# Starting the head inside layer 3 and feeding it chunk by chunk, in a Fourier-layer image kernel

## The chip, the cores and the metric

The kernel runs on one core of one Trainium2 chip. The metric is the device time of one execution in microseconds; the time given for the kernel before is the median of three executions.

## What is computed

The input is eight images of eight channels, 256 x 256 pixels, float32. Two residual layers follow each other; each normalises its input per group of channels first. The first is a Fourier neural operator in four groups (two input channels and ten hidden channels each), the second a 3 x 3 dilation. Cut to what matters:

```python
h = _gconv1x1(concat(x, grid), fc0_w, fc0_b)            # 4 groups: 2+2 -> 10 channels
for i in range(4):
    h1 = _spectral_conv(h, sp_w1[i], sp_w2[i])          # 24 x 12 low modes of a 2-d FFT
    h2 = _gconv1x1(h, w_w[i], w_b[i])                   # 10 -> 10 per pixel
    h = h1 + h2
    if i < 3: h = _gswish(h, betas[i])
h = _gswish(_gconv1x1(h, fc1_w, fc1_b), betas[3])       # "head": 10 -> 128 per pixel and group
y = _gconv1x1(h, fc2_w, fc2_b)                          # "head": 128 -> 2

x = x + L0(_gn(x))                                      # layer 0, above
x = x + L1(_gn(x))                                      # layer 1: max over 3 x 3 windows
```

## The kernel before

**Rows and chunks.** The 256 rows of an image are dealt as 128 pairs of rows, n = 0 to 127. A pair of 512 pixels sits in one of NBLK = 3 blocks of 10 channels on the partitions of a group, in one of NQ = 4 columns, of one of NCH = 11 chunks of the tile `h`. A *state* is one column of one chunk, 128 partitions x 512 numbers, and holds up to three pairs. There are 44 states for the 128 pairs. Before the change, `_row_of` deals pair n to column n // 32, chunk (n % 32) // 3 and block n % 3 within the 32; a state order that follows n therefore walks all 11 chunks of column 0 first, then all of column 1, and so on.

**Layers.** `layers` runs, for each image, four layers. A layer takes the spectrum (`spectrum_h`), multiplies the modes (`mix`, DVE), turns them into rows (`rows_of`, PE `p_g` at L465/L471), and then `layer` runs 11 bursts, one for each chunk: 48 matmuls into `p_z` (L550/L553 and L556) and two ACT evictions into `h` (L561, in layer 3 L563). Layers 0 to 2 also transform each chunk back (`turn` L504, `transform` L521 to L525, `gather` L535). Layer 3 instead stores each chunk to DRAM as soon as it is made (`stored[c]`, 1,024 KB, L565), and beside it the next image's first spectrum is worked out (the generator `side`, which is `start(b + 1)`: `spectrum_x`, then `mix` of layer 0).

**The head.** For each image, `head` returns `first` and `second`. A `first` step, written *f* here, takes one pair n: it loads the state three further on (`load_state`, L752, 256 KB, SP queue, four buffers), does four matmuls from `hs` into PSUM (L776, 32 rows deep) and two ACT evictions with Silu into `act` (L777 and L778). A `second` step, *c*, takes two pairs: eight matmuls from `act` (L793) into one PSUM bank; `sum_up` later adds that bank to the rows of the image `y` on DVE (L800 for the first of eight, L802 for the others). After every eighth *c* there are statistics (L805 or L808) and a store of the finished rows. An image has 128 *f* and 64 *c*. In this text f1.0 is the first step *f* of image 1.

**The tail.** After the 64th *c* of an image, its `dilate` generator is put into `tails`. Each call makes one small piece of DVE work. For each of eight bands of rows the pieces are: fetch of the band (`yin`, POOL queue, 512 KB, L829), nothing, first maximum `m` (L840, waits for the fetch), second maximum (L842), vertical maximum (L845, L846), and then the subtraction, residual sum and store (L849 to L857) together with the next band's fetch. `yin` has one buffer.

**The order is written out by hand.** Nothing is scheduled: every generator yields strings, and the main loop plays them. "f" and "c" are steps of the oldest head that has one left, "C" is a *c* whose sum is put off, "t" is one call of the tail. The engines run their instructions in exactly that order. In layer 3 each chunk yields "fct" (up to chunk 7, then "fc") and "f"; `REST` holds the five strings that are played between layer 3 of one image and layer 0 of the next, another set for image 0 than for the rest. When no head is left in the layers, a last loop plays "ffc" and one tail call until the last image's head is through:

```python
        while heads:
            for kind in "ffc":
                if heads:
                    step(kind)
            tail()
```

`ready` (L579, L580) marks three chunks of layer 3 after which the first three states are asked for, and the first rows of `y` with the second of them. `stored`, yielded after layer 3, puts the new head into `heads`; until then, in image 0, no head exists, and `alone[0]` is true. For the last image `y` and the dilation live in `h` itself (`ya`, in chunks 0 to 2, `ma` and `oa` behind it), since `h` is free by then; `head` clears the border of `ya` on POOL.

Of the kernel before, what the change touches and what calls it, by code (L numbers as in the profile page):

```python
# [33 lines left out]
NBLK = 3  # L34
NCH = 11
NQ = 4
# [3 lines left out]
DR = 2  # L40
STEPS = 128
BEHIND = mybir.DependencyInfo(mybir.DependencyClass.Sync, mybir.DependencyReason.DATA)
REST = ("ff", "f", "f", "fC", "fc"), ("f", "fc", "ffC", "ff", "fc")


@with_exitstack
def fno_dilate_kernel(ctx: ExitStack, tc: tile.TileContext, a: dict, out: bass.AP):
# [11 lines left out]
    def ps_a(name):  # L59
        return ps.tile([128, 512], F32, tag="one", bufs=2, name=name)  # L60
# [4 lines left out]
    def ps_four(name):  # L65
        one, tri = ps_a(f"{name}_0"), ps_tri(f"{name}_1")
        return one, tri, [one] + [tri[:, i, :] for i in range(3)]

    def part(i):
        return slice(32 * i, 32 * i + 32)  # L70
# [132 lines left out]
    alone = [True]  # L203
# [182 lines left out]
    def load_sw(l, k):  # L386
        t = sb.tile([128, G, 2 * WID, WID], F32, tag="sw", bufs=3)
        nc.sync.dma_start(t.rearrange("p g m i -> p (g m i)"), a["spw"][l, k])
        return t
# [102 lines left out]
    def read_x(b, c):  # L492
        if b < n_img:
            for g in range(G):
                nc.sync.dma_start(h[32 * g : 32 * g + 6, c].rearrange("p f w -> p (f w)"), a["xp"][b, c, g])

    def layer(b, l, out_, stored, side, ahead):
# [73 lines left out]
        if l == 3:  # L571
            for c in range(NCH):
                burst(c)
                yield "fct" if c < 8 else "fc"
                next(side, None)
                if c + 1 < NCH:
                    yield "f"
                next(side, None)
                if c in ((3, 4, 5) if alone[0] else (6, 8, 9)):  # L579
                    yield "ready"  # L580
                if 0 < c < 4 and b + 1 < n_img:
                    ahead.setdefault("sw", []).append(load_sw(0, c - 1))
                if c > 3 and not alone[0]:
                    read_x(b + 1, c - 4)
            return
        for k in range((NCH + 1) // 2):
            c = 2 * k
# [48 lines left out]
    def start(b, out_):  # L636
        if b < n_img:
            if b == 0:
                out_["sw"] = [load_sw(0, k) for k in range(3)]
            yield from spectrum_x(b, out_)  # L640
            yield from mix(b, 0, out_)

    def rest(b, then):
        c = 0 if b == 0 else NCH - 4
        for n, _ in enumerate(then):
            yield REST[b > 0][n]
            for _ in range(2 if b == 0 else 1):
                if c < NCH:
                    read_x(b + 1, c)
                    c += 1  # L650
        for i in range(c, NCH):
            read_x(b + 1, i)
# [67 lines left out]
    def now_or_later(f):  # L720

        if held[0] is None:
            f()
        else:
            held[0].append(f)
# [14 lines left out]
    def head(b, stored, stats):  # L740
        hs, acts, box, done = {}, {}, {}, [0, 0]
        last = b + 1 == n_img
        if last:
            for t in (ya[:, :, 0:1], ya[:, :, HW + 1 :], ya[:, 0, :], ya[:, 17, :]):
                nc.gpsimd.memset(t, -BIG)

        def load_state(k):

            if k < NQ * NCH:
                j, c = k // NCH, k % NCH  # L750
                hs[k] = sb.tile([128, PIX], F32, tag="hs", bufs=4, name=f"hs_{b}_{k}")
                now_or_later(lambda: nc.sync.dma_start(hs[k], stored[c][:, PIX * j : PIX * (j + 1)]))  # L752

        def load_y(t):

            if t < 8:
                if last:
                    y = ya[:, 1 + 2 * t : 3 + 2 * t, 1 : HW + 1]
                else:
                    y = sb.tile([128, 512], F32, tag="yp", name=f"y_{b}_{t}")  # L760
                    y = y.rearrange("p (s w) -> p s w", s=2)
                box[t] = y
                now_or_later(lambda: nc.sync.dma_start(
                    y, a["x"][b].rearrange("c (p t s w) -> (c p) t s w", p=16, t=8, s=2)[:, t]))

        def first():

            n = done[0]
            done[0] += 1
            if n % 32 % NBLK == 0:  # L770
                load_state(n // 32 * NCH + n % 32 // NBLK + 3)
            k, blk = n // 32 * NCH + n % 32 // NBLK, n % 32 % NBLK
            act = sb.tile([128, G, 512], F32, tag="act", bufs=4, name=f"act_{b}_{n}")
            one, tri, banks = ps_four(f"p_fc1_{b}_{n}")
            for g in range(G):
                mm(banks[g], w1[part(g), blk, :], hs[k][part(g), :], start=True, stop=True)  # L776
            nc.scalar.activation(act[:, 0, :], one, AF.Silu)  # L777
            nc.scalar.activation(act[:, 1:4, :], tri, AF.Silu)  # L778
            acts[n] = act

        def second():

            n = 2 * done[1]
            done[1] += 1
            t, rb = n // 16, n % 16
            if rb == 8:
                load_y(t + 1)
            y, acc = box[t], ps_a(f"p_fc2_{b}_{n}")
            sums = acc.rearrange("p (s w) -> p s w", s=2)
            for i in range(2):  # L790
                act = acts.pop(n + i)
                for g in range(G):
                    mm(acc[part(g), :], w2[:, g, 15 - rb - i : 47 - rb - i], act[:, g, :],  # L793
                       start=i == 0, stop=i == 1)
            sums_due.append(lambda: add(t, rb, y, sums))

        def add(t, rb, y, sums):

            if rb == 0:
                nc.vector.scalar_tensor_tensor(y, sums, b2, y, ALU.add, ALU.add)  # L800
            else:
                nc.vector.tensor_tensor(y, sums, y, ALU.add)  # L802
            if rb == 14 and last:
                for i in range(2):
                    nc.vector.bn_stats(stats[:, 2 * t + i, :], y[:, i])  # L805
                dilate_early(t)
            elif rb == 14:
                nc.vector.bn_stats(stats[:, t, :], y.rearrange("p s w -> p (s w)"))  # L808
                whole = y_rows[b % 2][:]
                nc.gpsimd.dma_start(  # L810
                    bass.AP(whole.tensor, whole.offset + (1 + 2 * t) * HW, [[16 * HW, 128], [HW, 2], [1, HW]]), y)

        def ahead(n):

            load_state(n)
            if n == 1:
                load_y(0)

        return done, first, second, ahead


# [38 lines left out]
    heads, tails = [], []  # L860
# [16 lines left out]
    def tail():  # L877
        if tails and next(tails[0], tails) is tails:
            tails.pop(0)

    stats_of = {}
    with tc.manual_schedule(engines={PE, DVE, ACT, SP}):
        d = {}
        for _ in start(0, d):
            pass
        for b in range(n_img):
            stored = [dram.tile([128, NQ * PIX], F32, tag=f"hs{c}", name=f"stored_{b}_{c}") for c in range(NCH)]
            nxt, new, n_ready = {}, None, 0
            for n in layers(b, stored, d, start(b + 1, nxt), nxt):
                if n == "ready":  # L890
                    if new is None:
                        if b + 1 < n_img:
                            stats_of[b] = sb.tile([128, 8, 6], F32, tag="bn_y", name=f"bn_y{b}")
                        else:
                            stats_of[b] = spare[:, 16384:16480].rearrange("p (n s) -> p n s", s=6)
                        new = head(b, stored, stats_of[b])
                    new[3](n_ready)
                    n_ready += 1
                elif n == "stored":
                    heads.append((b, new))  # L900
                    alone[0] = False
                else:
                    for kind in n or "":
                        if kind == "t":
                            tail()
                        elif heads:
                            step(kind)
            d = nxt
# [5 lines that stand above are left out]
        for t in tails:  # L914
            for _ in t:
                pass
# [7 lines left out]
def _row_of():  # L924

    rows = np.full((NBLK, NQ, NCH, 2), -1)
    for n in range(HW // 2):
        j, c, blk = n // 32, n % 32 // 3, n % 32 % 3
        rows[blk, j, c] = 16 * (n % 16) + 2 * (n // 16) + np.arange(2)
    return rows  # L930


# [147 lines left out]
```

## Time and profile before

| | us |
|---|---|
| median of three executions (lowest, highest) | 3749.41 (3743.65, 3750.35) |
| the profiled execution, device time | 3748.67 |
| its span, first to last instruction | 3746.9 |
| mean granted TensorE clock | 0.978 |
| layer 3 of image 0, first burst to last (PE) | 305.6 to 341.2 |
| head of image 0: first step f | 341.07 |
| last burst of image 7 ends, last loop begins | about 3441.6 |
| last step f starts | 3716.38 |

A table of groups gives the instructions by line; its first rows are the head: L778 ACT 1493.3 us, L776 PE 1133.8 us, L793 PE 1008.7 us, L777 ACT 616.5 us. Engines are PE (matmul), PEld (weight load), DVE, ACT and POOL; SP only issues DMAs. In a timeline, a line has the start, the duration, the engine, the source line, the operation, output and input tiles, and in brackets the idle time before it and who ended it. In a table of waits, a line has the waiting instruction, the one it waited for, the total, the number of waits and the longest.

### The profile page before, as it was taken

What the parts mean: (1) busy time and instruction counts of PE and PEld (TensorE: products, weight loads), DVE (VectorE), ACT (ScalarE), POOL (GpSimd) and SP (SyncE); (2) the same over time, 40 slices, a digit from 0 to 9 for tenths busy, and PEclk for the clock granted to TensorE, in tenths of its full rate; (3) what the DMA queues carried; (4) which work ended last, traced back from release to release, by engine and by line L of the source; (5) the groups of instructions that cost most, each with busy time, mean ns of one, the idle gap of its engine ahead of it and who ended that gap; (6) DMA issues with size and microseconds to landing.
All of it is one profiled execution on the core that took longest, in us unless ns stands there. A gap on an engine that the chain in (4) does not pass through costs nothing.

```text
span 3746.9 us, 117677 instructions
## 1 busy us (share of the span) xinstructions
PE 3526.2 (94%) x53432; PEld 1287.2 (34%) x53432; DVE 2412.8 (64%) x3753; ACT 2836.0 (76%) x2947; POOL 117.0 (3%) x202
## 2 busy tenths in 40 slices
PE   5768999999999999999999999999999999999997
PEld 2323333333333333333333333333333333333222
DVE  6776656557775667756776577765777566772543
ACT  2435878777778777887787877878787877788886
POOL 1000000000000000000000000000000000000000
PEclk7878999999999999999999999999999999999998
DMA  3005211442225222262123612244222522225221
GB/s 89 16 15 198 60 46 44 149 123 63 74 81 180 82 61 71 85 211 64 50 68 112 192 55 71 58 155 131 63 74 79 180 85 60 71 63 188 81 85 48
DMA packets 114067, 344.91 MB, mean 92 GB/s; under 512 B 15984, under 2 KB 18480, under 8 KB 98144
## 3 DMA queue, kind: packets, MB, share of 16 engines
q1 hardware_dynamic: 95392, 276.32, 24.3%
q0 software_dynamic: 18176, 61.07, 4.9%
q8 instruction: 420, 6.88, 0.8%
q14 instruction: 79, 0.65, 0.1%
HBM read 213.33 MB, written 123.74 MB: 90 GB/s over the span
## 4 chain that ended last, share of the span: by engine, by line
PE 72%; DVE 16%; issue 5%; ACT 5%; DMA 2%; POOL 0%; ACTq 0%; DVEq 0%; POOLq 0%
PE p_fc L793 19%; PE p_fc L776 18%; PE p_z L556 9%; PE p_z L553 7%; PE p_d L521 7%; PE p_z L550 3%; DVE y L802 3%; DVE turned L504 3%; PE p_u L535 3%; DVE S L402 3%; DVE turned L399 2%; PE p_g L471 2%; DMA yin<-y_rows 2%; DVE turned L360 1%; ACT act L778 1%
## 5 line engine op out<-in xcount | busy, mean ns | idle before, releaser
L778 ACT ACTIVATE act<-p_fc 128x1536 f32<-128x1536 f32 x1024 | 1493.3, 1458 | 0.0
L776 PE MATMUL p_fc<-hs,c_w 32*128 32x512 f32 x8192 | 1133.8, 625 | 41.8 <-DVE y L802 20.8
L793 PE MATMUL p_fc<-act,c_w 128*32 128x512 f32 x8192 | 1008.7, 600 | 0.2 <-ACT act L778 0.2
L777 ACT ACTIVATE act<-p_fc 128x512 f32<-128x512 f32 x1024 | 616.5, 602 | 323.0 <-PE p_fc L776 311.5
L504 DVE STREAM_TRANSPOSE turned<-h 128x1024 f32<-128x1024 f32 x528 | 632.5, 1225 | 182.9 <-ACT h L561 182.3
L561 ACT ACTIVATE h<-p_z 128x512 f32<-128x512 f32 (+1 forms) x528 | 511.9, 1022 | 223.9 <-PE p_z L556 223.9
L802 DVE TENSOR_TENSOR y<-p_fc,y 128x512 f32<-128x512 f32 x392 | 267.9, 683 | 530.7 <-PE p_fc L793 530.7
L776 PEld LDWEIGHTS p_fc<-hs,c_w 32*128 32x128 f32 x8192 | 356.5, 183 | 614.1 <-ACT act L777 253.3
L793 PEld LDWEIGHTS p_fc<-act,c_w 128*32 128x32 f32 x8192 | 222.0, 109 | 694.5 <-issue 317.2
L556 PE MATMUL p_z<-c_binv,zt 32*128 32x256 f32 x5632 | 409.6, 404 | 0.0
L553 PE MATMUL p_z<-h,c_wt 32*32 32x512 f32 x8448 | 373.5, 604 | 8.4 <-ACT act L777 4.2
L556 PEld LDWEIGHTS p_z<-c_binv,zt 32*128 32x128 f32 x5632 | 258.7, 186 | 309.2 <-issue 296.2
L521 PE MATMUL p_d<-turned,c_fw 32*32 32x480 f32 (+1 forms) x9216 | 308.7, 541 | 0.7 <-DVE turned L504 0.4
L525 ACT ACTIVATE turned<-p_d 128x1440 f32<-128x1440 f32 x144 | 182.9, 1270 | 90.7 <-PE p_d L521 87.5
L563 ACT ACTIVATE h<-p_z,c_bias 128x512 f32<-128x512 f32 (+1 forms) x176 | 186.5, 1110 | 76.1 <-PE p_z L556 75.9
L402 DVE TENSOR_REDUCE S<-turned 128x80 f32<-128x800 f32 x192 | 188.9, 984 | 5.9
L399 DVE TENSOR_TENSOR turned<-t,B 128x800 f32<-128x800 f32 x192 | 188.7, 983 | 0.9
L209 DVE COPY zt<-p_g 128x264 f32<-128x264 f32 x276 | 145.1, 614 | 63.8 <-PE p_g L471 36.5
L521 PEld LDWEIGHTS p_d<-turned,c_fw 32*32 32x32 f32 x9216 | 127.4, 103 | 166.0 <-issue 65.0
L360 DVE STREAM_TRANSPOSE turned<-zt 128x960 f32<-128x960 f32 x96 | 176.9, 1870 | 2.5
L553 PEld LDWEIGHTS p_z<-h,c_wt 32*32 32x32 f32 x8448 | 94.5, 103 | 187.8 <-DVE y L802 54.1
L535 PE MATMUL p_u<-turned,c_stack 128*32 128x480 f32 (+1 forms) x1152 | 136.7, 543 | 11.9 <-DVE turned L524 6.2
(186 smaller groups left out, 1715.5 us busy)
## 6 DMA issues: line engine op xcount, KB each, us to landing
stored<-h SPq DMA_DIRECT2D x88, 1024.0 KB
hs<-stored SPq DMA_DIRECT2D x352, 256.0 KB
t<-in_spw SPq DMA_DIRECT2D x96, 400.0 KB
yin<-y_rows POOLq DMA_DIRECT2D x56, 512.0 KB, 5.1
h<-in_xp SPq DMA_DIRECT2D x352, 48.0 KB
turned<-in_xw SPq DMA_DIRECT2D x16, 1024.0 KB
y<-in_x SPq DMA_DIRECT2D x56, 256.0 KB
y_rows<-y POOLq DMA_DIRECT2D x56, 256.0 KB, 3.9
```

Source lines behind the costliest of these rows:

```text
L399: nc.vector.tensor_tensor(pr, sw[k], bt[:, k2, k].unsqueeze(2).to_broadcast([128, G, 2 * WID, WID]), ALU.mult)
L402: nc.vector.tensor_reduce(s[k2][:, k].rearrange("p s o g -> p (s o) g"), pr.rearrange("p g m i -> p m g i"), AX.X, ALU.add,)
L504: nc.vector.transpose(dst[:, 2 * i : 2 * i + 2], h[:, c, 2 * i : 2 * i + 2].rearrange("p f (s x) -> p f s x", s=2))
L521: mm(banks[q][part(v % 4), : 240 * n], fw8[part(q), v, :], t[part(q), :, :, v, : NBLK * WID], start=v < 4, stop=v >= 4)
L553: mm(o, wt[part(q), l, g, :], h[part(q), c, f, :], start=True, stop=False)
L556: mm(banks[q][:, HW * s : HW * (s + 1)], zt[part(q), 2 * c + s].rearrange("p f o -> p (f o)"), binv[part(q), :], start=False, stop=s == 1)
L561: nc.scalar.activation(dst, src, AF.Silu)
L776: mm(banks[g], w1[part(g), blk, :], hs[k][part(g), :], start=True, stop=True)
L777: nc.scalar.activation(act[:, 0, :], one, AF.Silu)
L778: nc.scalar.activation(act[:, 1:4, :], tri, AF.Silu)
L793: mm(acc[part(g), :], w2[:, g, 15 - rb - i : 47 - rb - i], act[:, g, :], start=i == 0, stop=i == 1)
L802: nc.vector.tensor_tensor(y, sums, y, ALU.add)
```

## The change

`place(n)` deals the pairs: three to a state, twelve to a chunk for chunks 0 to 9, and the last eight, two to a state, to chunk 10. `_row_of`, `load_state` and `first` use it, so the head walks all four columns of chunk 0, then of chunk 1, and so on; it needs chunk c only from pair 12c on. The host's tables follow `_row_of`. `ready` comes after chunks 2, 3 and 4 in every image (before: 3, 4, 5 in image 0 and 6, 8, 9 in the others). The head is put into `heads` at the first `ready` (after chunk 2), in image 0 at the third (after chunk 4) with two steps *f* at once, no longer at `stored`. `REST` is one set for all images.

```diff
-REST = ("ff", "f", "f", "fC", "fc"), ("f", "fc", "ffC", "ff", "fc")
+REST = "f", "fc", "ffC", "ff", "fc"
+def place(n):
+    full = NBLK * NQ * (NCH - 1)
+    if n < full:
+        return divmod(n, NBLK)
+    k, blk = divmod(n - full, 2)
+    return NQ * (NCH - 1) + k, blk
...
-                if c in ((3, 4, 5) if alone[0] else (6, 8, 9)):
+                if c in (2, 3, 4):
                     yield "ready"
...
-            yield REST[b > 0][n]
+            yield REST[n]
...
-                j, c = k // NCH, k % NCH
+                c, j = k // NQ, k % NQ
...
-            if n % 32 % NBLK == 0:
-                load_state(n // 32 * NCH + n % 32 // NBLK + 3)
-            k, blk = n // 32 * NCH + n % 32 // NBLK, n % 32 % NBLK
+            k, blk = place(n)
+            if blk == 0:
+                load_state(k + 3)
...
                     new[3](n_ready)
                     n_ready += 1
+                    if n_ready == (1 if b else 3):
+                        heads.append((b, new))
+                        if b == 0:
+                            step("f")
+                            step("f")
                 elif n == "stored":
-                    heads.append((b, new))
                     alone[0] = False
...
-        j, c, blk = n // 32, n % 32 // 3, n % 32 % 3
-        rows[blk, j, c] = 16 * (n % 16) + 2 * (n // 16) + np.arange(2)
+        k, blk = place(n)
+        rows[blk, k % NQ, k // NQ] = 16 * (n % 16) + 2 * (n // 16) + np.arange(2)
```

## The prediction

> **What bounds the kernel now.** I read the page first: busy times, the slices, the chain. Then PE's waits from 372 to 3440 us, then three stretches one by one.
>
> ```profile
> PE 3526.2 (94%) x53432; PEld 1287.2 (34%) x53432; DVE 2412.8 (64%) x3753; ACT 2836.0 (76%) x2947; POOL 117.0 (3%) x202
> ...
> PE   5768999999999999999999999999999999999997
> ...
> PE 72%; DVE 16%; issue 5%; ACT 5%; DMA 2%; POOL 0%; ACTq 0%; DVEq 0%; POOLq 0%
> ```
>
> PE is the bound. Its free time lies in the first three slices (image 0, layers 0 to 2, where no head can exist) and hardly anywhere else. The change does not reach those slices: before chunk 4 of layer 3 of image 0 its order is the old one. So it moves work from the last loop into a place that already has a 9 or 8.
>
> ```profile
> PE p_fc L776 <- DVE y L802: 20.6, 40, 1.8
> PE p_fc L776 <- DVE turned L524: 5.7, 6, 1.4
> PE p_u L535 <- DVE y L800: 4.8, 6, 1.2
> PE p_z L553 <- DVE y L802: 1.6, 6, 0.3
> ```
>
> These are the main waits of the seven later images that DVE causes. The last three come six times, once for each image whose layers carry a dilation; they will matter below. No wait of PE names a state load (`hs`) or a store.
>
> **What the change moves.** I compared the order in which both built programs issue on PE. The multiset of matmuls is the same. From the first spectrum matmul of image 1 on, the head is 14 *f* and 7 *c* ahead of its old place: 20 *f* and 9 *c* between chunk 4 of image 0 and `p_f` of image 1, where 6 and 2 stood. One image's cycle holds 128 *f* before and after, so the lead is carried unchanged through all images, and the last loop has 57 full rounds of f, f, c in place of 64. The sum is therefore: seven rounds at the end, against 14 *f* and 7 *c* in image 0, and what the shift does to DVE between.
>
> **Gain at the end.** The last loop's rounds:
>
> ```profile
> 3499.30 2.02 PE L776 MATMUL p_fc<-hs,c_w 32*128 32x512 f32 x16
> 3501.25 2.26 PE L793 MATMUL p_fc<-act,c_w 128*32 128x512 f32 x16
> 3503.44 2.02 PE L776 MATMUL p_fc<-hs,c_w 32*128 32x512 f32 x16
> ```
>
> Start to start 4.14 us; seven rounds are 29.0 us. Three rounds of the loop are late because eighth *c*, statistics and a piece of the dilation meet on DVE (they start 5.2, 7.9 and 5.3 us apart, 6.0 us lost). The tail now has four calls done when the loop begins, and by counting rounds I get four such meetings, one a shorter piece: +1 us (0 left: -6; one more at the mean of 2: +3). Gain at the end: 28.
>
> **Cost in image 0.** This is the step that decides. Two stretches, both from the end of chunk 4's burst in layer 3 to `p_f` of the next image: image 0 before, and image 1 before, which holds 20 *f* and 10 *c* among the same bursts and spectrum steps.
>
> ```profile
> core 0: us, PE busy (x) PEld busy (x) DVE busy (x) ACT busy (x) POOL busy (x), PEclk, DMA share, GB/s
> 321.76:354.83 33.07, 31.60 (x433) 12.67 (x429) 20.13 (x37) 25.82 (x27) 0.00 (x0) 1.00 0.91 360
> 736.36:796.15 59.79, 57.36 (x672) 19.88 (x664) 25.09 (x45) 51.02 (x54) 1.31 (x2) 1.00 0.68 210
> ```
>
> Image 0 after is image 1 before less one *c*. A *c* is 1.87 us here (eight matmul pairs, start to next start), so 57.9 us; less 33.07 is 24.8 us of cost. The free PE time in 33.07 us is only 1.47 us; the rest of what is regained comes from ACT pace, seen next: four *f* in a row went at 1.83 us each, where *f* with *c* between goes at 1.07.
>
> ```profile
> 343.50 1.61 PE L776 MATMUL p_fc<-hs,c_w 32*128 32x512 f32 x8 [0.31 <-ACT h L563]
> 345.33 1.61 PE L776 MATMUL p_fc<-hs,c_w 32*128 32x512 f32 x8 [0.22 <-ACT act L778]
> ```
>
> The two steps put in by hand are again *f* after *f*: +0.8.
>
> [...]
>
> **The first state.** The wait that the change adds: f0.0 needs state 0, which is loaded on SP's queue behind three stores of 1,024 KB and a 400 KB load; the trace has no load this close behind its store. The stores begin at 313.6 us and the DMA moves some 400 GB/s there (360 in the row, share 0.91), so 3.6 MB end at about 323, and the 256 KB state at 323.5 plus its completion; f0.0 is due at 325.0. Estimate +1 us, from 0 to 2.6 (one store at that rate). Queued behind f0.0 on PE is the burst of chunk 5, whose eviction releases the next store; nothing else waits for it.
>
> **Edits costed at nothing.** The order of states: the 352 loads keep size and number and are asked for three states (nine *f*) ahead; if that cover went, each would cost part of a store's 2.6 us. The earlier loads pass in front of some stores and `in_xp` loads on SP; the buffers they need were last read by PE a chunk earlier, so SP is not held up. In later images states 2 and 3 change places on SP; both are asked for at chunk 4, over a chunk before they are due. The last image's four border clears go to POOL (3% busy) four chunks earlier and wait there for the stores of chunks 0 to 2; `y` is loaded behind them. `REST` for image 0 is what the other images play already and is in the second row.
>
> **What the shift does to DVE.** This is the unknown part. The 45 calls of a dilation now start in layer 3 and stand four calls further on at each place. Where fetch and first maximum fall on the first and third call of one group of chunks, DVE stands in its queue:
>
> ```profile
> 1083.99 0.69 DVE L856 TENSOR_TENSOR o<-o,yin 128x512 f32<-128x512 f32 x1
> ...
> 1090.47 1.22 DVE L840 TENSOR_TENSOR m<-yin 128x1024 f32<-128x1024 f32 x1 [2.97 <-DMA yin<-y_rows]
> ...
> 1093.54 1.01 PE L535 MATMUL p_u<-turned,c_stack 128*32 128x480 f32 x8 [0.74 <-DVE y L800]
> ```
>
> Queued behind L840 are two transposes and the sum that frees a PSUM bank; PE waits 0.74 us for that, so some 2.2 of the 2.97 us are covered. Before, an image has one such place (layer 2) and a looser one (layer 1: DVE 1.97, PE 1.38 us). Counting calls through DVE's order, after it has two of the tight kind, in layers 0 and 1, and no looser one. The three rows of waits above sum to 12.1 us; in their place I put 6 x 2 x 0.8 = 9.6 (4.8 us over six): -2.5 us. Bounds: nothing left, -12.1; each at the longest of such waits, 1.4, is 16.8: +4.7. I take the tight row, since the order is the same instruction by instruction.
>
> [...]
>
> **Sum.** -29.0 + 1 + 24.8 + 0.8 + 1 - 2.5 = -3.9. On the profiled execution, 3748.67, that is 3744.8; its time stands 0.7 below the median. I say 3745. Bounds: -29.0 - 6 + 24.8 - 12.1 = -22 and -29.0 + 3 + 24.8 + 0.8 + 2.6 + 4.7 = +7, hardly ever reached together.
>
> **Rivals.**
> 1. *DVE's stalls go away* (the fetch lands in time at its new places): -3.9 - 9.6 = -13.5, 3735. For it: L840 waited for its fetch only 13 times out of 56. Against: the new places are as tight as the one that waits 2.97. Chance 0.17.
> 2. *The head falls into idle PE time*: 28 us, 3721. For it: weight loads are busy 12.67 and ACT 25.82 of 33.07 us. Against: the second stretch. Chance 0.06.
> 3. *The tight stalls pass to PE* (slower): the twelve new ones meet a fetch that lands 7.5 us after the end of L856, as the looser one in layer 1 did (964.2 to 971.76 us), in place of 5.8 (1084.7 to 1090.47); DVE then stands 4.6 us, 2.4 beyond the cover. 12 x 2.4 = 28.8 for 9.6: +15, 3764. It is slower beyond doubt once each costs PE over 1.75 us. For it: fetches of both lengths are in the trace. Against: 2.97 cost only 0.74. Chance 0.13.
> 4. *Head and stores collide in every image*: state 0 late by one store in eight images, 8 x 2.6 - 4 = +17, 3766; in images 1 to 7 two chunk periods of 6.7 us lie between the load and its use. Chance 0.03.
> That the head does not start earlier at all is excluded by the order on PE.
>
> **Chances.** The forecast has 0.61. About 0.2% (7.5 us) is what a measurement of this kernel can tell from no change. Below 3741.9 lie rivals 1 and 2 and some 0.06 of the forecast: 0.29. Above 3756.9 lie rivals 3 and 4: 0.15, since 0.01 of them stays below. The rest is 0.56. The forecast's own range is 3738 to 3752; to leave out 2 in 10 it must reach rival 1 and half of rival 3: 3733 to 3760.
>
> **What would show it.** The first burst after chunk 4 of image 0, to `p_f` of image 1, takes 57 to 61 us; the last loop has seven rounds fewer at 4.14; f0.0 starts near 325 to 328. L840 waits for `yin` some 3 us in layers 0 and 1, twice in each image, with PE waits near 0.8. PE's busy time stays near 3526. Wrong would be: a wait of PE for `hs`, PE waits for DVE far from 10 us in the rows above, or a cycle of an image far from the 443 us of now ((3441.6 - 341.1) / 7).

## The result and the profile after

| | before | after |
|---|---|---|
| median of four executions each, side by side (lowest, highest), us | 3746.53 (3741.40, 3750.35) | 3775.97 (3771.78, 3779.37) |
| profiled execution, us | 3748.67 | 3775.83 |
| its span, us | 3746.9 | 3773.7 |
| mean granted TensorE clock | 0.978 | 0.969 |

The ratio after to before is 1.0065, with a 95% interval from 1.0049 to 1.008: the change makes the kernel slower by 0.65%, some 24 us (the two medians are 29 us apart, which lies inside the interval). The forecast was 3745, and 3776 lies above its range.

The page of the changed kernel, three lines that answer to those of before (busy times with instruction counts, TensorE's slices, the chain that ended last):

```profile
PE 3544.7 (94%) x53432; PEld 1302.4 (35%) x53432; DVE 2413.3 (64%) x3753; ACT 2836.5 (75%) x2947; POOL 117.0 (3%) x202
...
PE   5767999999999999999999999999999999999997
...
PE 54%; issue 31%; DVE 9%; ACT 3%; DMA 2%; POOL 0%; DVEq 0%; ACTq 0%; POOLq 0%
```

The first line already points to the answer. TensorE runs 53432 matmuls as before, but is busy 3544.7 us where it was 3526.2: the same matmuls take 18.5 us longer, while DVE, ACT and POOL are as busy as they were to within 0.5 us. Of the 26.8 us that the span grew, two thirds are not idle time at all.

To see where, I cut the span at the prediction's own marks. First image 0, from the end of chunk 4's burst in layer 3 to `p_f` of image 1 (changed kernel; the columns are the stretch, its length, busy time and instructions of each engine, the granted clock, and the DMA):

```profile
core 0: us, PE busy (x) PEld busy (x) DVE busy (x) ACT busy (x) POOL busy (x), PEclk, DMA share, GB/s
323.10:386.43 63.33, 58.52 (x656) 20.66 (x652) 25.35 (x45) 51.15 (x55) 0.58 (x1) 0.97 0.64 221
```

Then all of images 1 to 7, from that `p_f` to the last burst, in the kernel before

```profile
354.83:3441.60 3086.77, 3020.92 (x46528) 1103.51 (x46528) 2038.56 (x3102) 2453.31 (x2545) 92.63 (x155) 1.00 0.31 95
```

and in the changed one:

```profile
386.43:3496.70 3110.27, 3041.29 (x46528) 1118.84 (x46527) 2040.24 (x3106) 2454.96 (x2545) 93.35 (x156) 0.99 0.31 94
```

| stretch | before | after | difference | forecast |
|---|---|---|---|---|
| image 0, chunk 4 to `p_f` of image 1 | 33.07 | 63.33 | +30.3 | +26.6 |
| images 1 to 7, `p_f` to last burst | 3086.77 | 3110.27 | +23.5 | -2.5 |
| last burst (3440.59; 3495.72) to last *f* (3716.38; 3743.20) | 275.8 | 247.5 | -28.3 | -28 |
| sum | | | +25.5 | -3.9 |

The remaining 1.3 us of the span lie outside these stretches. The trade that the prediction was mostly about, image 0 against the last loop, came out within 4 us of its forecast. What went wrong stands in the middle row: images 1 to 7 issue the same 46528 matmuls, and these are busy 20.4 us longer (3041.29 - 3020.92).

The waits of TensorE in that stretch of the changed kernel (waiting instruction, what it waited for, total, times, longest):

```profile
PE p_fc L785 <- DVE y L811: 20.8, 41, 1.8
PE p_g L480 <- DVE zt L218: 13.0, 14, 0.9
PE p_u L544 <- DVE y L811: 7.5, 12, 1.3
PE p_sv_y L235 <- DVE zt L218: 5.0, 6, 0.8
```

All its waits together are 60.4 us, where before they were 57.1 over the same stretch. So waits explain 3.3 of the 23.5 us. But one row is new: `p_sv_y`, a one-column matmul of the finished image's statistics, now stands at the start of layer 0 of images 2 to 7 and waits 0.84 us each time. What stands around it there, in the order of time (start, duration, instruction, and in brackets the idle time before it):

```profile
1287.79 1.03 PE L785 MATMUL p_fc<-hs,c_w 32*128 32x512 f32 x7
1289.66 0.35 PE L235 MATMUL p_sv_y<-mv_y,c_grp 128*128 128x1 f32 x2 [0.84 <-DVE zt L218]
1289.94 1.47 PE L559 MATMUL p_z<-h,wcn 6*32 6x512 f32 x32
1291.34 1.53 PE L565 MATMUL p_z<-c_binv,zt 32*128 32x256 f32 x16
1292.80 2.03 PE L559 MATMUL p_z<-h,wcn 6*32 6x512 f32 x32
1294.76 2.09 PE L565 MATMUL p_z<-c_binv,zt 32*128 32x256 f32 x16
1296.63 1.93 PE L785 MATMUL p_fc<-hs,c_w 32*128 32x512 f32 x8
...
1300.47 1.14 PE L785 MATMUL p_fc<-hs,c_w 32*128 32x512 f32 x8
```

And the same microseconds in windows of 1.2 us, where the column behind POOL is the granted clock:

```profile
1290.40:1291.60 1.20, 1.20 (x36) 0.36 (x32) 1.00 (x7) 0.44 (x1) 0.00 (x0) 1.00 0.83 174
1291.60:1292.80 1.20, 1.20 (x16) 0.54 (x12) 0.98 (x7) 0.00 (x0) 0.00 (x0) 0.65 0.57 213
1292.80:1294.00 1.20, 1.20 (x36) 0.30 (x32) 0.00 (x0) 1.13 (x2) 0.00 (x0) 0.50 0.00 0
...
1297.60:1298.80 1.20, 1.20 (x12) 0.20 (x8) 0.00 (x0) 1.20 (x2) 0.00 (x0) 0.50 0.06 14
1298.80:1300.00 1.20, 1.20 (x16) 0.24 (x8) 0.00 (x0) 1.20 (x3) 0.00 (x0) 1.00 0.00 0
```

The same place in the kernel before, where the burst of layer 0 follows the head directly:

```profile
1252.56 1.03 PE L776 MATMUL p_fc<-hs,c_w 32*128 32x512 f32 x7
1253.52 2.02 PE L550 MATMUL p_z<-h,wcn 6*32 6x512 f32 x32
1255.48 1.15 PE L556 MATMUL p_z<-c_binv,zt 32*128 32x256 f32 x16
1256.55 1.19 PE L550 MATMUL p_z<-h,wcn 6*32 6x512 f32 x32
```

Sixteen `p_z` matmuls take 2.09 us in the changed kernel; in the kernel before the same sixteen took 1.15. Nothing is waited for: the engine is busy all through, at half its clock, for 6.8 us, and then the clock is whole again. I call such a piece a *half-clock stretch* (some of the expectations below call it a spell and give it 3.6 us, three windows of 1.2 us; the clock's records in the trace give 3.41). From 320 us on, without the idle end of the span (the last 23 to 25 us), the kernel before has two, 3.41 us each; the changed one has thirteen, 68 us together. They last 3.41 us or two or three times that. Four of the thirteen stand at the start of layer 0 right behind a `p_sv_y`; three more in the rest of an image (where `REST` is played) behind a wait of 1.80 us for `y`; one in image 0 behind the wait of 2.39 us for `hs`. Of the other five, two follow waits of 1.07 and 2.32 us, and three follow no recorded wait.

The lines of before also show that the wait at the start of layer 0 is only in part new. There the first 32 `p_z` matmuls take 2.02 us and the next 32 take 1.19: the first three start 0.45 us apart, so TensorE stands there too, but the records overlap and a table of waits does not list it. From the end of the last `p_fc` to the first matmul that reads `zt` it is 1.88 us before and 2.52 us after. So what the statistics add to each image is 0.64 us (3.9 us over six), and not the listed 0.84 (5.0); the rest was counted as busy time before.

### The profile page after: what moved, and what is told of

It reads as the page before. It is cut to its first block, busy times and chain, and to the rows that moved or that the text cites. A ratio compares the mean times of both kernels' runs of the same rounds, so it can differ in the third digit from the quotient of the medians.

```text
span 3773.7 us, 117577 instructions
## 1 busy us (share of the span) xinstructions
PE 3544.7 (94%) x53432; PEld 1302.4 (35%) x53432; DVE 2413.3 (64%) x3753; ACT 2836.5 (75%) x2947; POOL 117.0 (3%) x202
## 4 chain that ended last, share of the span: by engine, by line
PE 54%; issue 31%; DVE 9%; ACT 3%; DMA 2%; POOL 0%; DVEq 0%; ACTq 0%; POOLq 0%
PE p_fc L802 17%; PE p_fc L785 17%; PE p_z L565 6%; PE p_z L562 5%; PE p_d L530 5%; DVE y L811 2%; PE p_u L544 2%; PE p_z L559 2%; DMA yin<-y_rows 2%; DVE S L411 1%; DVE turned L408 1%; DVE turned L513 1%; ACT act L786 1%; ACT act L787 1%; PE p_b L378 1%
## 5 line engine op out<-in xcount | busy, mean ns | idle before, releaser
L785 PE MATMUL p_fc<-hs,c_w 32*128 32x512 f32 x8192 | 1146.8, 628 | 39.7 <-DVE y L811 22.6
L785 PEld LDWEIGHTS p_fc<-hs,c_w 32*128 32x128 f32 x8192 | 365.8, 184 | 603.3 <-ACT act L786 243.3
L565 PE MATMUL p_z<-c_binv,zt 32*128 32x256 f32 x5632 | 418.6, 412 | 0.0
L218 DVE COPY zt<-p_g 128x264 f32<-128x264 f32 x276 | 145.2, 612 | 63.7 <-PE p_g L480 36.5
```

Of the source, the lines that this page charges most:

```text
L565: mm(banks[q][:, HW * s : HW * (s + 1)], zt[part(q), 2 * c + s].rearrange("p f o -> p (f o)"), binv[part(q), :], start=False, stop=s == 1)
```

## The experiments

The theory (A): the shift puts the dilation's statistics at a place where TensorE waits shortly among matmuls of few rows; the clock drops behind such a wait, and the loss is several times the wait. The first rival (B): half-clock stretches come from the head's own earlier place. The second (C): they come by chance. All ratios below are to runs of the kernel before on the same chip, with a 95% interval.

**1. The dilation kept at its old place.** The changed kernel, but a finished head's dilation joins the tails only after layer 3:

```diff
-    heads, tails = [], []
+    heads, tails, waiting = [], [], []
...
-                    tails.append((dilate if b + 1 < n_img else dilate_last)(b, stats_of.pop(b)))
+                    (waiting if b + 1 < n_img else tails).append((dilate if b + 1 < n_img else dilate_last)(b, stats_of.pop(b)))
...
                 elif n == "stored":
+                    tails.extend(waiting)
+                    waiting.clear()
```

> The changed kernel, but a finished head's dilation waits until layer 3 has ended before it joins the tails, so that all its pieces stand at their old places; the head's early start stays. Theory A (the extra time is spells of half TensorE clock, set off where the dilation's statistics now stand): 3740 to 3750 us, mean clock 0.976 to 0.979, few spells after image 0. Theory B (the spells come from the head's own earlier place, its loads beside the stores and its new phase in the layers): 3768 to 3780, clock 0.969. Theory C (the spells fall by chance after any change of order): anything between, with no relation to the place of the statistics.

Measured: 3750.15 us, ratio 0.9998 [0.9987, 1.0009], clock 0.976 in the profiled run, five half-clock stretches. The whole loss is gone with the head still starting early, so B falls as a cause by itself. What is left of the change is worth nothing that can be measured; the prediction's sum without its term for DVE, -1.4 us, fits that.

**2. Only the dilation moved.** The kernel before, with four tail calls more between layer 3 and layer 0, so that the dilation stands as in the changed kernel while the head does not:

```diff
-REST = ("ff", "f", "f", "fC", "fc"), ("f", "fc", "ffC", "ff", "fc")
+REST = ("ff", "f", "f", "fC", "fc"), ("f", "fct", "ffCt", "fft", "fct")
```

> The kernel before, with four calls of the tail put between layer 3 and layer 0 of images 1 to 7, so that every piece of a dilation stands four calls on, as in the changed kernel, and the second statistics matmul again stands between the rows and burst 0 of layer 0; the head stays at its old place. Theory A: 3760 to 3776, clock 0.970 to 0.974, spells of 3.6 us or multiples in layer 0 behind that matmul. Theory B: 3744 to 3750, clock 0.978. Theory C: between.

Measured: 3759.58, ratio 1.0018 [1.0006, 1.003], clock 0.974, eight stretches, six of them behind the six `p_sv_y`. Part of the loss comes without any other part of the change, and the stretches come with that place. That they are what costs here is not shown: in the profiled execution (the fastest of ten) TensorE is busy 3523.2 us, 3 less than before, although 34 us of images 1 to 7 are at half clock, and this order has a wait that the changed kernel does not have, `p_st_y` for ACT, six times, 6.5 us. Run 1 and run 2 do not add up to the changed kernel either: 0 and 0.18% against 0.65%.

**3. The wait for the first state taken away.** In image 0 the first states are asked for one chunk earlier:

```diff
-                if c in (2, 3, 4):
+                if c in ((1, 3, 4) if alone[0] else (2, 3, 4)):
```

> The changed kernel, with image 0's first state asked for after chunk 1 in place of chunk 2. Both theories: the wait of 2.4 us for hs at the first step f of image 0 and the spell of 3.6 us after it go, 3770 to 3774; all else as in the changed kernel.

Measured: 3771.84, ratio 1.0045 [1.0029, 1.0062]. The wait of 2.39 us and the stretch behind it are gone; of the seven stretches that are left, four again stand behind `p_sv_y`. Its interval overlaps that of the changed kernel, so the few us of this edit are not told apart from nothing.

**4. The statistics one call earlier.** `p_sv_y` moves from the start of layer 0 into layer 3; the call that it leaves is empty, so that the dilation's bands stay where the change puts them:

```diff
         yield
-        yield
         q = ps_tri(f"p_sv_{name}")[:, 0, :]
...
+        yield
```

> The changed kernel, with the second statistics matmul one tail call earlier (in layer 3, behind chunk 7) and an empty call in its old place; the eight bands stand as in the changed kernel. Theory A: the four spells (32 us at half clock, so 16 us) and the six waits of 0.8 us at the start of layer 0 go, 3753 to 3762, clock about 0.973. Theory B and C: 3768 to 3780.

Measured: 3761.43, ratio 1.0028 [1.0017, 1.004], eight stretches. Two at the start of layer 0 are left, and the burst there starts as in the kernel before (1.88 us). By the middle values more than half of the loss, 14 of 24 us, belongs to this one matmul's place, where it delayed TensorE by 3.9 us.

**5. A filler that missed.** Two dead matmuls were put ahead of `p_sv_y` so that TensorE has work while it waits:

```diff
-        q = ps_tri(f"p_sv_{name}")[:, 0, :]
+        tri = ps_tri(f"p_sv_{name}")
+        q = tri[:, 0, :]
+        for i in range(2):
+            mm(tri[:, 1 + i, :HW], ident, binv, start=True, stop=True)
```

> The changed kernel with two dead matmuls (128x256 columns each) put on TensorE just before the p_sv_y matmul of every image, where it waits 0.84 us for zt at the start of layer 0; their product is read by nobody. Theory A (the loss is the clock gate's, set off by that wait among work of few rows): fewer than two of the six images show a half-clock stretch behind p_sv_y (four did), the mean granted clock rises to .971 to .975, and the time falls to 3758 to 3770 although work was added. Rival (the wait costs only its own length and the half-clock stretches come by chance): 3774 to 3782, as many stretches as before. A second rival: the filler keeps the engine busy but the statistics still come as late, so time 3770 to 3777 with fewer stretches.

Measured: 3778.92, ratio 1.0065 [1.0045, 1.0085], ten stretches, three behind the statistics. That reads like the rival's number, but the trace shows that the filler (L237) did not fill. One such place of it:

```profile
1288.64 1.10 PE L237 MATMUL p_sv_y<-c_binv,ident 128*128 128x256 f32 x4 [0.84 <-DVE zt L218]
1289.37 0.41 PEld L238 LDWEIGHTS p_sv_y<-mv_y,c_grp 128*128 128x128 f32 x2
1289.58 0.28 PE L238 MATMUL p_sv_y<-mv_y,c_grp 128*128 128x1 f32 x2
```

It waits the 0.84 us itself. The wait is not for the statistics but for the PSUM tile, whose last reader is the copy L218 of `p_g` to `zt`. So this run tells nothing of A against the rival, but it tells what to change next. Of the cause that the expectation names under theory A, the traces show the granted clock alone, 0.50 in a stretch, and nothing of what sets it.

**6. The same order, another bank.** `p_sv_y` goes to the pool of single banks; every engine issues in the changed kernel's order:

```diff
-        q = ps_tri(f"p_sv_{name}")[:, 0, :]
+        q = ps_a(f"p_sv_{name}")
```

> The changed kernel, same order on every engine, but p_sv's result goes to a bank of the pool of single banks and not to one of the pool of three, whose last reader (the copy of p_g to zt) it waited 0.84 us for at the start of layer 0. Theory A (that wait, among work of few rows, sets off the half-clock stretches): the wait is gone, at most two of the six images show such a stretch there, ratio to the kernel before 1.001 to 1.004 (3752 to 3765), clock over .972. Rival A2 (not the wait, but that the engine has less to do from there on, or the statistics' place in itself): stretches and time as in the changed kernel, ratio 1.005 to 1.008, clock .968 to .970. If the single bank makes it wait as long, nothing is told.

Measured: 3761.14, ratio 1.0022 [1.0012, 1.0031], clock 0.972. This group of its waits, over 372 to 3460 us, stands in the place of the 5.0 us on `p_sv_y`:

```profile
PE p_z L559 <- DVE mv_y L239: 2.5, 6, 0.4
```

The listed wait is halved, to 0.42 us, not gone: the burst's tile now waits for the reader of `p_sv_y`. The delay up to the first matmul that reads `zt` is nearly gone, 1.91 us where the changed kernel has 2.52. So 3.7 us of delay in six images went, and the ratio fell by 0.0043, 16 us; the two intervals do not meet. Of the six starts of layer 0, two still have a stretch. In all the profile has thirteen, as many as the changed kernel, but 48 us in place of 68. A2 falls: with the statistics at the same place in the same order, it is how long they hold TensorE up that decides.

**7. Only the wait.** The kernel before, plus one column of matmul, read by nobody, into the pool of three banks at the start of layer 0 of images 2 to 7:

```diff
+            if l == 0 and k == 0 and b > 1:
+                mm(ps_tri(f"p_no_{b}")[:, 0, 0:1], grp, grp[:, 0:1], start=True, stop=True)
             burst(c)
```

> The kernel before with one thing added: a matmul of one column, read by nobody, at the start of layer 0 of images 2 to 7, into the pool of three banks, so that TensorE waits there as p_sv_y does in the changed kernel. Without a clock effect it costs six waits of 0.84 us and six short matmuls, 6 to 8 us: ratio 1.0016 to 1.0022, clock .975 to .978. Theory A: besides that, half-clock stretches behind it in three or more of the six images, some 10 to 18 us more: ratio 1.004 to 1.007, clock .970 to .973.

Measured: 3766.97, ratio 1.0036 [1.0024, 1.0049], a little under A's 1.004 and above the 1.0016 to 1.0022 that the waits alone would cost. In the profile, which is of the slowest of the six executions (3769.55, clock 0.970; the others 0.972 to 0.974), all six are followed by 6.8 us at half clock, and there are nine stretches in all. One of the six:

```profile
2156.05 0.35 PE L590 MATMUL p_no<-c_grp 128*128 128x1 f32 x2 [0.84 <-DVE zt L209]
2156.33 1.27 PE L550 MATMUL p_z<-h,wcn 6*32 6x512 f32 x32
2157.54 1.99 PE L556 MATMUL p_z<-c_binv,zt 32*128 32x256 f32 x16
2159.46 2.04 PE L550 MATMUL p_z<-h,wcn 6*32 6x512 f32 x32
```

Its waits for `zt` sum to 5.1 us and its matmuls to about 2 (twelve records, 0.25 us each, overlapping). Up to the first matmul that reads `zt` it is 2.33 us, 0.45 more than before, so the delay that was added is 2.7 us in six images, while the ratio is worth 13.5 us (0.0036 x 3751).

**8. Only the dealing of rows.** The kernel before with `place` and the states' order, the head starting at `stored`:

```diff
-                j, c = k // NCH, k % NCH
+                c, j = k // NQ, k % NQ
...
+            k, blk = place(n)
+            if blk == 0:
+                load_state(k + 3)
```

> The kernel before with only the dealing of rows and the states' order taken from the change; the head still begins once all is stored, its states taken in chunk order. Theory A: nothing that sets off a half-clock stretch is moved, so the time is the kernel before's, ratio 0.999 to 1.001 (3745 to 3752), clock .976 to .979, at most 5 half-clock stretches. Rival (the dealing itself costs, by loads or border rows): 3755 or more.

Measured: 3746.89, ratio 0.9988 [0.9977, 1.0], five stretches, clock 0.976. The dealing costs nothing, as the prediction had it.

**9 to 11. A version that beats both.** The wait of 1.8 us behind `y`, in the rest of seven images (six in the kernel before), is the largest that is left, and stretches follow it too. Six of DVE's mixing operations stand between two sums there. The side work is dealt so that four do. Run 9 is run 1 with the edit of run 3, for comparison; run 10 adds the dealing; run 11 has the dealing alone, in the kernel before:

```diff
-        for n, _ in enumerate(then):
+        for n, ahead in enumerate((0, 0, 3, 1, 1) if b + 1 < n_img else ()):
+            for _ in range(ahead):
+                next(then)
             yield REST[n]
```

> The changed kernel with the finished head's dilation kept at its old place (as in e1_old_tail) and, for image 0 alone, the head's first states allowed one step sooner behind their stores (as in e3_state_sooner), which took the 2.4 us wait for hs away. Theory A: e1's time less 2.4 and less the half-clock stretch of 1.7 us behind it: ratio to the kernel before 0.997 to 0.9995 (3740 to 3748). Rival (the wait only moves to later states, or the head's start stops image 0's tail): ratio 1.000 to 1.003.

> As e7_old_tail_sooner, and the side work handed out around the head's rest is dealt more evenly, so that four and not six of VectorE's mixing operations stand between the two sums of the rest that TensorE waits on. Theory A: the wait of 1.8 us behind y in the rest of seven images falls under 1 us and its half-clock stretches are gone: 5 to 9 us less than e7, 3732 to 3742, clock .979 to .981. Rival (VectorE sets the rest's length whatever the order): the wait moves to the next sum and the time is e7's within 3 us.

> The kernel before with only the more even dealing of side work in the rest of images 1 to 6 (as in e8_rest_even), nothing of the change. If the gain of e8 over e7 is the rest's alone: six waits of 1.8 us behind y shrink to under 0.4, ratio 0.996 to 0.998 (10 to 12 us less than the kernel before, with the half-clock stretches behind those waits). If e8 needs the change for it: ratio 0.998 to 1.000.

Measured, in this order: 3747.18, ratio 0.9988 [0.9976, 1.0001]; 3734.95, ratio 0.9954 [0.9937, 0.9972]; 3741.62, ratio 0.997 [0.9957, 0.9984]. The waits of run 10 show what went (the 5.0 us of `p_sv_y` are absent, as in run 1):

```profile
PE p_g L480 <- DVE zt L218: 13.0, 14, 0.9
PE p_fc L789 <- DVE y L815: 11.3, 42, 0.4
```

The longest wait behind `y` fell from 1.8 to 0.4 us. Run 10 is 12 us below run 9, more than the 5 to 9 that I expected, and has no stretch in any rest (two stretches in all, run 9 six, run 11 four); it is the fastest of all. Run 11 gives most of it without the change. That the change adds the rest, 0.9954 against 0.997, is not shown, since the intervals overlap.

**Chance, counted.** Rival C is not wholly wrong: stretches at the start of layer 0 come without a listed wait as well. Counted in images 2 to 7 of each profiled run:

| listed wait there | stretches in six images | together |
|---|---|---|
| 0.84 us: changed kernel, runs 2, 3, 5, 7 | 4, 6, 4, 3, 6 | 23 of 30 |
| 0.42 us: run 6 | 2 | 2 of 6 |
| none: before, runs 1, 4, 8, 9, 10, 11 | 0, 1, 2, 1, 4, 2, 3 | 13 of 42 |

The place is prone to it; the wait raises it from about a third to about three quarters. That is a count over single profiles, which are of the fastest execution in runs 2 and 3 and of the slowest in run 7.

The traces say what the chance is. In each of the thirteen, all stretches begin on one grid with steps of 3.413 us, to within 0.01 us from the first to the last, so where a piece of work falls against that grid matters. Of the 42 starts of layer 0 without a listed wait, those 13 have a stretch whose first matmul of 6 rows starts between 0.91 us ahead of a grid line and 0.29 us behind one, and none of the other 29 starts lies there: 1.2 of 3.41 us is the third. Of the 24 in the changed kernel and runs 2, 3 and 7, the four without a stretch start 0.43 to 0.87 us ahead of a line, and none of the other 20 does. So the longer delay does not make stretches at random; it leaves fewer safe places. Images of one run are not separate trials: in run 7 an image takes about 447.15 us, 131 steps, and images 5, 6 and 7 start at the same place to within 0.02 us.

The clock of every execution goes with its time: 71 of the kernel before, on three chips, have a mean clock of 0.975 (0.971 to 0.978) and take 3742 to 3764 us; within each chip 0.001 less clock goes with 2.7 to 2.9 us more. The changed kernel's four have 0.968 to 0.970.

## Why the prediction was wrong

- **The cost in image 0** was right in its main part: +30.3 us against 26.6. Of the 3.7 us that are missing, 1.4 are the first state, whose wait was 2.39 us, inside its bounds of 0 to 2.6 but above the +1 I took (the DMA, put at some 400 GB/s, moved 357 GB/s from 318 to 323 us and 369 from there to f0.0 at 328.76); behind it stood a half-clock stretch of 3.4 us, worth up to 1.7 (half its length, an estimate), that no term had.
- **The gain at the end** was right: 28.3 us against 28. Seven rounds fewer, each as long as before (4.14 us from start to start, 3734.93 to 3739.07 us in the changed kernel).
- **Edits costed at nothing** held: run 8 shows it for the dealing and the order of states. No wait for `hs` besides the first appears in the changed kernel.
- **What the shift does to DVE** is the step that failed: its term was -2.5 us, within -12.1 and +4.7, and images 1 to 7 took +23.5. It failed in two ways. Its count of calls was right for what it counted: `p_u` waits 12 times, 7.5 us in all, where the twelve tight places were put at 9.6. But it looked only at the calls that fetch and take maxima. The same generator begins with two matmuls of statistics, and the shift puts the second in front of the first burst of layer 0, where it takes a PSUM tile still being read. The term puts that at nothing; it is 5.0 us in the list of waits and 3.9 us of delay. With it the listed waits changed by +3.3 us in place of -2.5.
- The larger miss is in the price. The step, and the sum, charge a wait of TensorE with its own length. The runs show that the matmuls behind it must be charged too: 20.4 us of matmul time in images 1 to 7, against 3.3 us of waiting. Run 6 takes 3.7 us of such delay away and wins 16 us; run 7 adds 2.7 us of it alone and loses 13.5. The mean clock stood in the table of times, at 0.978, and no step of the sum used it. The sign that the prediction had named for this, a busy time of TensorE near 3526 us, did fail: it is 3544.7.
- **Rival 3**, tight stalls that pass to PE, named the right sign and a nearby time, 3764, for another reason: fetches landing late. `p_u` waits at most 1.3 us in the changed kernel, so that reason did not come about.

What stays open: how the remaining 0.2% of run 6 over run 1 divides between its 0.42 us waits, the twelve waits of `p_u` and the stretches elsewhere; and why the dilation's shift costs 0.18% alone and 0.65% with the head's early start. Whether what drops the clock is idle time as such or how few rows the matmuls use was not tried by itself either, but the thirteen traces speak for the second. Cut into steps of the grid from 360 to 3440 us, they hold 11,587 steps at full clock, of which 77 are followed by half clock. Count each matmul as rows in x rows out x columns, spread over its recorded time: all 77 do less than half of the median step's work, as only 298 steps do, and 76 of them are among the 200 with the least. By recorded idle time they do not stand out: 28 of the 77 have none (overlapping records can hide some), and 248 steps with 0.84 us or more are followed by full clock.

## What to carry to other kernels

When TensorE is the bound, compare its busy time before and after for the same number of matmuls (3526.2 and 3544.7 us for 53432 here), ahead of any list of waits: if it grew, look for windows with a lower granted clock and read what stands just before each. Price a new wait on TensorE not at its length alone but with up to half of a possible half-clock stretch behind it, above all where matmuls of few rows follow: in run 7, with matmuls of 6 rows, 2.7 us of delay cost 13.5 us, and the stretches were 3.41 us or a multiple. Look for waiting in matmuls that take longer than their like, too, since a list of waits leaves it out (2.02 us for 32 where the next 32 took 1.19). A small matmul of a side generator is a wait like any other, and the PSUM tile that it takes may be what it waits for, as `p_sv_y` did for 0.84 us. When work is shifted against other work, list every instruction of the shifted generator on every engine, not only those of the engine that it mostly uses.

## What was not expected of the hardware

A listed wait of 0.84 us was followed by 6.8 us at half clock in all six cases of run 7, while most of the waits of 1.8 us for `y` were followed by none: three of seven in the changed kernel and one of six in the kernel before were. From 320 us on, the length of the stretches was always 3.41 us or two or three times that, and in each of the thirteen traces they began on a fixed grid of that step. No idle time near these stretches was longer than 2.5 us (2.39 in the changed kernel), and a third of the layer-0 starts without a listed wait (13 of 42) have a stretch too. Run 7 puts 0.45 us of delay more (2.33 us where it was 1.88) ahead of the matmuls with 6 rows, and all six of its images have a stretch there, where the profile of the kernel before has none.

The stretches cost less than half their length: in images 1 to 7 the changed kernel has 61 us at half clock and the kernel before 3.4, which would be 29 us of lost matmul time if every matmul took twice as long; the busy time grew by 20.4. Some 3.3 us must be added to that, an estimate: the first 32 `p_z` of layer 0 hold standing time in both kernels, 2.02 us before and 1.47 after, and six times that difference left the busy time. In run 2 the price was far below half, as said there.
